# Sums of attention weights over four steps in every group, one of them by an adding transfer

## The chip, the cores and the metric

One core of a Trainium2 chip runs the kernel. The core has a matrix engine (TensorE, PE), a vector engine (VectorE, DVE), an activation engine (ScalarE, ACT), a general one (GpSimd, POOL) and a queue for transfers (SyncE, SP). Each works through its own list of instructions in order; semaphores tell one engine when another's result is there. The metric is device time in microseconds, the median of several executions.

## The reference

The input has 16 batches of 1024 nodes with 256 features and one adjacency matrix. Three graph-attention layers and one transformer layer follow each other, each with a layer norm and a rectifier ahead of it and a residual around it. The change lies in the transformer layer's attention, which has 8 heads of 32 features:

```python
scores = jnp.einsum('fnhd,fmhd->fhnm', q, k) / jnp.sqrt(jnp.asarray(D, x.dtype))
mask = (adj > 0)[None, None, :, :]
scores = jnp.where(mask, scores, jnp.asarray(-1000000000.0, x.dtype))
attn = jax.nn.softmax(scores, axis=-1)
t = jnp.einsum('fhnm,fmhd->fnhd', attn, v).reshape(F, N, C)
```

Layer norm, a two-layer network (256 to 256 to 256) and a second layer norm follow. A softmax needs, beside the weighted sum of the values, the sum of the weights of each row. That sum is what the change computes in another way.

## The kernel before, in words

`direct` writes the whole program down first and orders it afterwards. Each piece of work (some matmuls, an activation, a transfer) is recorded with its engine, an estimated duration, and the buffers that it reads and writes (`Record.add`). `Record.schedule` then plays these estimates through: for each engine it takes, of the pieces whose inputs are ready, the one with the lowest key. The key of a piece is its batch number plus a value interpolated in `KNOTS` at the piece's place in its stream, so that pieces of different batches and layers interleave: while one batch is in its attention, the next is in its graph layers and the one before in its feed-forward part. `PASS` is the time that a result is taken to need from one engine to the next. A transfer is recorded with two numbers: how long it occupies the transfer engines and how much later it lands; `SLACK` is added to that. These numbers only decide the order in which instructions stand in the engines' lists. The chip keeps that order and goes by its semaphores.

In `attention` (from L1084), for each of two groups of four heads (`g`), each half of the rows (`hf`) and each of eight column tiles (`jt`), one step does this:

- PE multiplies queries and keys, one matmul a head, into four score banks (L1355). Queries and keys come as high and low parts through DRAM (`project`, L1134 to L1158: an `hl` buffer is stored, then read back in four transfers).
- ACT takes the exponential of each head's scores into `pa` (L1379), a buffer with two heads side by side, 128 x 1024 elements; a step fills two of them, and six exist.
- DVE multiplies each by the adjacency mask (L1388).
- PE adds weights times values into one bank: a quad of four matmuls, one a head, each on a quarter of the array's columns (L1220, `bank<-pa,va`).
- For the sums of the weights PE multiplies the weights by a block of ones into another bank: again a quad (L1220, `bank<-sums,ones`).

The last item need not be done for each step, as weights of several steps can be added first. `run_of` gives the number of steps: 1 in the last batch, in which nothing is added; elsewhere 4 for the second half of the rows and 2 for the first. With 2, DVE adds the two steps' weights into a buffer `sums` (L1247, two additions of 128 x 1024) and one quad follows. With 4, DVE adds the first two, and for the third and the fourth step a transfer each, issued by POOL, adds the weights to `sums` in SBUF (L1256, two transfers of 512 KB a step; the fourth's waits for the third's on the same `sums`). Then comes the quad.

At the end of a batch (`feed`) the residual is read from DRAM into `xr` (L1505), the second layer norm's result is added, and the sum is stored. These transfers, the queries' and keys', and the graph layers' rows all stand in SP's one list. Names in the profile: `qs` and `ks` are queries and keys, `sc` a score bank, `va` the values, `pt`, `row` and `qb` belong to the graph layers (L870, L897, L984), `xh` holds a batch's features.

Of the kernel before, what the change touches and what calls it, by code (L numbers as in the profile page):

```python
# [113 lines left out]


WEIGHT = {"pe": 1.0, "dve": 0.3}
PASS = {"pe": 0.122, "act": 0.556, "dve": 0.232, "pool": 0.13, "dma": 0.0}


class Work:  # L120
# [23 lines left out]
class Record:  # L144
# [135 lines left out]


BEHIND, HELD = 2.0, 1.35
SLACK = 0.722
KNOTS = {
    "gat0": (-10.926, -10.742, -7.218, -4.626, -2.628, -2.099, -0.444, -3.636, -2.816),
    "gat1": (0.191, 0.25, 0.454, 0.45, 0.566, 0.582, 0.633, 1.016, 0.672),
    "gat2": (1.126, -0.076, -0.221, -0.062, 0.894, -0.428, 0.959, 1.018, 1.17),
    "beside": (1.093, 3.374, 4.836, 2.176, 5.971),
    "values": (1.444, -1.53, -3.682, -3.253, 0.902, 0.891, 2.874, 0.851, 0.421),
    "steps": (0.98, 1.188, 1.323, 1.512, 1.578, 1.712, 2.006, 2.02, 1.489),  # L290
    "feed": (2.026, 2.163, 1.768, 1.658, 2.343, 1.828, 2.009, 2.223, 3.042),
    "last": (3.521, -0.495, 0.103, 1.329, 1.339, 5.969, 5.585, 3.41, 5.439),
}
BIAS = 2.241
LEAD = {"act": 8.212, "dve": 0.635}

SWITCH = {
    ("full", "col4"): 0.137,
# [11 lines left out]
def tt_us(n):  # L310
    return (n / 0.96 + 67) / 1000
# [17 lines left out]
def direct(ctx, tc, flag, x, adj, gat_w, gat_a, w_qkv, ln1_g, ln1_b, ln2_g, ln2_b, w1, b1, w2, b2, out):  # L329


    nc = tc.nc
    NB, N, C = x.shape
# [92 lines left out]
    def dve(us, emit, w, r):  # L426
        rec.add("dve", us, emit, w, r)
# [4 lines left out]
    def dma(moved, lands, emit, w, r, key=None, us=0.57, engine="dma"):  # L432
        rec.add(engine, us, emit, w, r, key=key, moved=moved, lands=lands)
# [293 lines left out]
    def gat(xt, b_mv, b_rstd, l, my):  # L727
# [120 lines left out]
        def spread(hf, h, rd):  # L848

            row = my.row.new()  # L850
            dma(
                1.2,
                2.07,
                lambda: nc.sync.dma_start(
                    row.t,
                    rd.t[h * TH : (h + 1) * TH, :]
                    .rearrange("t n -> (t n)")
                    .partition_broadcast(P),
                ),
                [row],  # L860
                [rd],
            )
            return row
# [220 lines left out]
    def attention(b, xt, b_mv, b_rstd):  # L1084
# [42 lines left out]
        def project(g, hf, keys, stack, at):  # L1127

            sc, hi, lo = r_sc.new(), r_hi.new(), r_lo.new()
            c0 = keys * C + g * P  # L1130

            def product():
                for ct in range(CT):
                    nc.tensor.matmul(  # L1134
                        sc.t,
                        wqkv_sb[:, ct, c0 : c0 + P],
                        hT.t[:, ct, hf * HALF : (hf + 1) * HALF],
                        start=ct == 0,
                        stop=ct == CT - 1,
                    )  # L1140

            pe(CT * mm_us(HALF), product, [sc], [b_qkv] + [hT((ct, hf)) for ct in range(CT)])
            act(act_us(HALF), lambda: nc.scalar.copy(hi.t.bitcast(F32R), sc.t), [hi], [sc])  # L1143
            dve(
                tt_us(HALF),
                lambda: nc.vector.tensor_sub(lo.t, sc.t, hi.t),
                [lo],
                [sc, hi],
            )
            hl = r_hl.new()  # L1150
            for k, part in enumerate((hi, lo)):
                dma(0.65, 1.5, lambda: nc.sync.dma_start(hl.t[:, k, :], part.t), [hl(k)], [part])
            for a in range(4):
                k = ((0, 0, 1, 1), (0, 1, 0, 1))[keys][a]
                dma(
                    1.0,
                    1.83,
                    lambda: nc.sync.dma_start(  # L1158
                        stack.t[a * D3 : (a + 1) * D3, :, at : at + HALF],
                        hl.t[:, k, :].rearrange("(r d) n -> d r n", r=HG),  # L1160
                    ),
                    [stack((r, hf if keys else 0, a)) for r in range(HG)],
                    [hl(k)],
                )
# [62 lines left out]

        def run_of(g, hf):

            return 1 if b == NB - 1 else 4 if hf == 1 else 2  # L1230

        rec.stream(b, KNOTS["steps"])
        GROUP = 2
# [1 line left out]
        for n in range(len(steps) + LAG):  # L1235
            m = n - LAG
            if m >= 0:
                g, hf, jt = steps[m]
                if jt == 0:
                    accs[g, hf] = [r_bank.new(), r_bank.new()]  # L1240
                run = run_of(g, hf)
                if jt % run == 1:
                    sums[g, hf] = [r_sums.new() for _ in range(2)]
                    for ss, p0, p1 in zip(sums[g, hf], pas[m - 1], pas[m]):
                        dve(
                            tt_us(2 * HALF),
                            lambda: nc.vector.tensor_add(ss.t, p0.t, p1.t),  # L1247
                            [ss],
                            [p0, p1],
                        )  # L1250
                elif jt % run:
                    for ss, pt in zip(sums[g, hf], pas[m]):
                        dma(
                            2.8,
                            0.85,
                            lambda: nc.gpsimd.dma_start(ss.t, pt.t, accum_op=ALU.add),  # L1256
                            [ss],
                            [pt],
                            us=1.135,
                            engine="pool",  # L1260
                        )
                pe(
                    0.8585,
                    lambda: quad(
                        accs[g, hf][0],
                        lambda r: pas[m][r // 2].t[:, r % 2, :],
                        lambda r: va.t[:, jt, (g * HG + r) * D3 : (g * HG + r + 1) * D3],
                        jt == 0,
                        jt == NT - 1,
                    ),  # L1270
                    [accs[g, hf][0]],
                    pas[m] + [va(jt)],
                    ("col4", "col4"),
                )
                if jt % run == run - 1:
                    ss = pas[m] if run == 1 else sums[g, hf]
                    pe(
                        0.8585,
                        lambda: quad(
                            accs[g, hf][1],  # L1280
                            lambda r: ss[r // 2].t[:, r % 2, :],
                            lambda r: ones,
                            jt == run - 1,
                            jt == NT - 1,
                        ),
                        [accs[g, hf][1]],
                        ss,
                        ("col4", "col4"),
                    )
# [111 lines left out]
    def feed(b, x3, hn):  # L1401
# [95 lines left out]
        def back(hf):  # L1497
            yT = yTs[hf]
            for it in (hf * TH, hf * TH + 2):
                g, z, mvz, rstdz = r_bank.new(), r_fz.new(), r_mvz.new(), r_rstdz.new()  # L1500
                xr = r_xr.new()
                dma(
                    1.0,
                    1.83,
                    lambda: nc.sync.dma_start(xr.t, x3.t[:, it : it + 2, :]),  # L1505
                    [xr(0), xr(1)],
                    [x3(hf)],
# [763 lines left out]
```

## Time and profile before

| | |
|---|---|
| Median of 3 runs | 4077.2 us (4068.3 to 4077.9) |
| Profiled execution, device time | 4072.0 us |
| Its span, first to last instruction | 4070.3 us |
| PE busy | 4012.3 us, 99% |
| DVE busy | 3501.7 us, 86% |
| ACT busy | 2666.6 us, 66% |
| POOL busy | 621.0 us, 15% |
| DMA engines, mean rate | 112 GB/s |
| TensorE clock granted | 0.995 |

The profile is one execution. Its page gives busy time and share of the span for each engine; "PEld" is PE's loading of weights, which overlaps its matmuls. Groups of instructions are named by source line, engine and operation, with what they write and read, the count, busy time in microseconds, the mean of one in nanoseconds, and then the engine's idle time just before them and what ended most of it. Matmuls in fp32 appear as two records each. The ends of matmuls are modelled, so times from one start to the next say more of PE than durations. The chain of waits is followed back from the last instruction, at each step to what released it.

### The profile page before, as it was taken

Reading aid. Unit: us, or ns where it says so; the run is one execution under the profiler, and the core shown is the slowest. Engines: PE = TensorE matmul, PEld = TensorE weight load, DVE = VectorE, ACT = ScalarE, POOL = GpSimd, SP = SyncE. Lnnn points to the kernel's source line nnn. Section 1 sums busy time; section 2 is a strip of 40 time slices with the busy share of each in tenths; the row PEclk is TensorE's granted clock in tenths of the full one; section 3 lists DMA queues with packets and bytes.
Section 4 is the critical chain, followed back from the end, with each engine's and each line's share of the span. In section 5 each row is a group of like instructions: output and inputs, shape, how many; then the busy total and the mean of one; then the engine's idle time right before and its main releaser. Section 6 shows DMA issues by size and latency. Waiting matters only on the chain.

```text
span 4070.3 us, 66071 instructions
## 1 busy us (share of the span) xinstructions
PE 4012.3 (99%) x23874; PEld 2352.0 (58%) x23874; DVE 3501.7 (86%) x5994; ACT 2666.6 (66%) x6673; POOL 621.0 (15%) x631
## 2 busy tenths in 40 slices
PE   7999999999999999999999999999999999999998
PEld 4566466564655646566564665646556465665643
DVE  7778898989989899898988989899898998989866
ACT  5467575775757767576675766757577675766765
POOL 1101111111111112111111111111111121111200
PEclk9999999999999999999999999999999999999999
DMA  3034454444545345463444544445543454624451
GB/s 128 27 103 115 126 126 109 113 104 115 124 125 123 83 117 126 115 150 76 126 110 123 127 110 113 104 115 122 127 121 82 117 128 115 150 69 121 112 137 51
DMA packets 227520, 456.54 MB, mean 112 GB/s; under 512 B 24688, under 2 KB 59760, under 8 KB 227184
## 3 DMA queue, kind: packets, MB, share of 16 engines
q1 hardware_dynamic: 192624, 326.39, 28.3%
q0 software_dynamic: 34560, 125.84, 16.2%
q8 instruction: 190, 3.11, 0.3%
q14 instruction: 146, 1.20, 0.1%
HBM read 225.25 MB, written 101.06 MB: 80 GB/s over the span
## 4 chain that ended last, share of the span: by engine, by line
PE 94%; DMA 3%; ACT 1%; DVE 1%; issue 0%; SPq 0%; DVEq 0%; ACTq 0%; POOLq 0%
PE bank L897 21%; PE bank L1220 16%; PE sc L1355 12%; PE bank L984 11%; PE bank L772 9%; PE bank L531 6%; PE sc L1134 5%; PE bank L1452 5%; PE bank L994 5%; PE sc L1172 3%; DMA sums<-pa 2%; PE sc L531 1%; DVE pt L870 1%; ACT waste L448 0%; ACT pa L1379 0%
## 5 line engine op out<-in xcount | busy, mean ns | idle before, releaser
L1388 DVE TENSOR_TENSOR pa<-pa,mask 128x1024 f32<-128x1024 f32 x1024 | 1222.7, 1219 | 166.1 <-ACT pa L1379 162.6
L1379 ACT ACTIVATE pa<-sc 128x512 f32<-128x512 f32 x2048 | 1101.6, 611 | 370.1 <-DVE sums L1247 174.4
L870 DVE SCALAR_TENSOR_TENSOR pt<-row,e,mask 128x512 f32<-128x512 f32 x1472 | 1011.9, 744 | 46.6 <-DMA row<-rd 27.7
L897 PE MATMUL bank<-qb,pt 128*128 128x257 f32 x4096 | 941.0, 380 | 0.0
L897 PEld LDWEIGHTS bank<-qb,pt 128*128 128x128 f32 x4096 | 770.6, 190 | 143.6 <-issue 20.1
L1355 PE MATMUL sc<-qs,ks 128*128 128x512 f32 x2048 | 727.9, 457 | 2.6 <-DMA hl<-hi 1.1
L1220 PE MATMUL bank<-pa,va 128*32 128x512 f32 x4096 | 515.0, 597 | 0.0
L1355 PEld LDWEIGHTS sc<-qs,ks 128*128 128x128 f32 x2048 | 361.3, 189 | 237.9 <-ACT pa L1379 82.5
L984 PE MATMUL bank<-pt,qb 128*32 128x512 f32 x3840 | 461.7, 596 | 6.5 <-DVE pt L870 6.5
L1247 DVE TENSOR_TENSOR sums<-pa,pa 128x1024 f32<-128x1024 f32 x360 | 434.1, 1220 | 16.7 <-PE bank L1220 14.2
L772 PE MATMUL bank<-w_aug,hT 128*128 128x259 f32 (+1 forms) x1504 | 373.3, 389 | 0.0
L1256 POOL DMA_DIRECT2D sums<-pa x240 | 211.5, 883 | 954.1 <-DVE pa L1388 426.6
L772 PEld LDWEIGHTS bank<-w_aug,hT 128*128 128x128 f32 x1504 | 280.3, 190 | 99.6 <-ACT qb L794 35.4
L925 ACT ACTIVATE ex<-bank,rec 128x256 f32<-128x256 f32 x256 | 121.4, 475 | 288.9 <-DVE rec L917 288.7
L984 PEld LDWEIGHTS bank<-pt,qb 128*32 128x32 f32 x3840 | 116.5, 110 | 294.8 <-issue 219.5
L1220 PEld LDWEIGHTS bank<-pa,va 128*32 128x32 f32 x4096 | 115.0, 109 | 250.6 <-issue 225.7
L994 PE MATMUL bank<-pt,e 128*32 128x512 f32 x1920 | 252.0, 593 | 0.1
L1134 PE MATMUL sc<-hTa,wqkv_sb 128*128 128x512 f32 x512 | 240.0, 596 | 0.0
L468 POOL TENSOR_TENSOR rstd<-rstd,neg_half 128x4 f32<-128x4 f32 x96 | 169.2, 1762 | 362.1 <-DVE rstd L460 362.0
L1143 ACT CAST hi<-sc 128x512 fp32r<-128x512 f32 x128 | 75.1, 587 | 211.8 <-PE sc L1134 122.0
L502 ACT ACTIVATE hn<-xh,mv,rstd 128x256 f32<-128x256 f32 x376 | 202.8, 613 | 7.5 <-DVE mv L492 4.1
L1220 PE MATMUL bank<-sums,ones 128*32 128x512 f32 x1440 | 200.5, 600 | 3.9 <-DMA sums<-pa 3.7
(152 smaller groups left out, 4501.0 us busy)
## 6 DMA issues: line engine op xcount, KB each, us to landing
sums<-pa POOLq DMA_DIRECT2D x240, 512.0 KB, 6.0
ks<-hl SPq DMA_DIRECT2D x256, 256.0 KB
qs<-hl SPq DMA_DIRECT2D x256, 256.0 KB
row<-rd SPq DMA_DIRECT2D x184, 256.0 KB
hl<-hi SPq DMA_DIRECT2D x128, 256.0 KB
hl<-lo SPq DMA_DIRECT2D x128, 256.0 KB
xh<-in_x_dram SPq DMA_DIRECT2D x32, 512.0 KB
x<-xh SPq DMA_DIRECT2D x32, 512.0 KB
```

The costliest lines, as they stand in the source:

```text
L531: nc.tensor.transpose(dst(k), src(k), ident[:shape, :shape])
L772: nc.tensor.matmul(g.t[:, : C + 3 * H], hT.t[:, ct, k * P : (k + 1) * P], w_aug[l][:, ct, :], start=ct == 0, stop=ct == CT - 1,)
L870: lambda: nc.vector.scalar_tensor_tensor(pt.t, row.t, e3[:, 2, jt // TH, h, jt % TH : jt % TH + 1], mask[:, jt, hf * HALF : (hf + 1) * HAL ...
L897: nc.tensor.matmul(g.t[:, : D + 1], pts[jt].t[:, k * P : (k + 1) * P], qb[:, jt, 0, :], start=jt == 0, stop=jt == NT - 1,)
L984: nc.tensor.matmul(g.t[u * D + d : u * D + d + D3, :], qb[:, j, h + u, d : d + D3], pts[u][j - jt].t, start=j == 0, stop=j == NT - 1,)
L994: nc.tensor.matmul(gd.t[c : c + D3, :], one(jt + k, h + u).to_broadcast([P, D3]), pts[u][k].t, start=jt == 0, stop=jt == NT - 2,)
L1134: nc.tensor.matmul(sc.t, wqkv_sb[:, ct, c0 : c0 + P], hT.t[:, ct, hf * HALF : (hf + 1) * HALF], start=ct == 0, stop=ct == CT - 1,)
L1220: nc.tensor.matmul(ac.t[r * D3 : (r + 1) * D3, :], columns(r), of_head(r), start=first, stop=last,)
L1247: lambda: nc.vector.tensor_add(ss.t, p0.t, p1.t),
L1355: nc.tensor.matmul(scs[r - r0].t, ks.t[:, r, jt * P : (jt + 1) * P].bitcast(F32R), q.t[:, r, :].bitcast(F32R), start=True, stop=True,)
L1379: lambda: nc.scalar.activation(pt.t[:, v, :], sc.t, AF.Exp, scale=1.0 / math.sqrt(D3)),
L1388: lambda: nc.vector.tensor_mul(pt.t, pt.t, mask[:, jt : jt + 1, i0 : i0 + HALF].to_broadcast([P, 2, HALF]),),
```

## The change

Three things change in the program.

1. `run_of` gives 4 in every batch but the last, for both halves of the rows. The first half no longer goes in pairs.
2. In a run of 4, the first two steps are added by DVE as before, the third step's weights by an adding transfer as before, and the fourth step's weights by DVE, to the same `sums`, when the transfer has landed. The fourth step's transfer is gone.
3. The scheduler's numbers are fitted anew: `PASS`, `SLACK`, all `KNOTS`, `BIAS`, `LEAD`, and the two numbers of five kinds of transfer. They move instructions in the engines' lists and add none.

In the order as built, the matmul instructions with ones on summed weights go from 720 to 480 (each is two records in the profile), DVE's additions for the sums from 360 to 480, and the adding transfers stay at 240. The lists of all engines differ over their whole length.

```diff
-PASS = {"pe": 0.122, "act": 0.556, "dve": 0.232, "pool": 0.13, "dma": 0.0}
+PASS = {"pe": 0.146, "act": 0.223, "dve": 0.215, "pool": 0.13, "dma": 0.0}
...
-SLACK = 0.722
+SLACK = 0.871
 KNOTS = {
...
-    "values": (1.444, -1.53, -3.682, -3.253, 0.902, 0.891, 2.874, 0.851, 0.421),
-    "steps": (0.98, 1.188, 1.323, 1.512, 1.578, 1.712, 2.006, 2.02, 1.489),
-    "feed": (2.026, 2.163, 1.768, 1.658, 2.343, 1.828, 2.009, 2.223, 3.042),
-    "last": (3.521, -0.495, 0.103, 1.329, 1.339, 5.969, 5.585, 3.41, 5.439),
+    "values": (-0.174, -0.634, -1.621, -1.921, -0.925, 0.988, 7.017, 0.066, 0.002),
+    "steps": (0.679, 1.306, 1.313, 1.627, 1.731, 1.892, 2.245, 2.072, 0.464),
+    "feed": (2.531, 3.778, 2.14, 2.018, 2.622, 2.047, -0.257, 0.785, 3.186),
+    "last": (1.057, 1.904, 1.664, 0.156, 2.035, 2.203, 2.695, 3.982, 5.043),
 }
-BIAS = 2.241
-LEAD = {"act": 8.212, "dve": 0.635}
+BIAS = 2.353
+LEAD = {"act": 5.778, "dve": -2.572}
...
             dma(
-                1.2,
-                2.07,
+                1.45,
+                1.75,
                 lambda: nc.sync.dma_start(
                     row.t,
...
-                dma(0.65, 1.5, lambda: nc.sync.dma_start(hl.t[:, k, :], part.t), [hl(k)], [part])
+                dma(0.82, 1.67, lambda: nc.sync.dma_start(hl.t[:, k, :], part.t), [hl(k)], [part])
...
                 dma(
-                    1.0,
-                    1.83,
+                    1.15,
+                    2.18,
                     lambda: nc.sync.dma_start(
                         stack.t[a * D3 : (a + 1) * D3, :, at : at + HALF],
...
         def run_of(g, hf):
 
-            return 1 if b == NB - 1 else 4 if hf == 1 else 2
+            return 1 if b == NB - 1 else 4
...
+                elif run == 4 and jt % run == 3:
+                    for ss, pt in zip(sums[g, hf], pas[m]):
+                        dve(
+                            tt_us(2 * HALF),
+                            lambda: nc.vector.tensor_add(ss.t, ss.t, pt.t),
+                            [ss],
+                            [pt],
+                        )
                 elif jt % run:
                     for ss, pt in zip(sums[g, hf], pas[m]):
                         dma(
-                            2.8,
-                            0.85,
+                            2.4,
+                            2.0,
                             lambda: nc.gpsimd.dma_start(ss.t, pt.t, accum_op=ALU.add),
...
                 dma(
-                    1.0,
-                    1.83,
+                    1.3,
+                    1.6,
                     lambda: nc.sync.dma_start(xr.t, x3.t[:, it : it + 2, :]),
```

## The prediction

> **What bounds the kernel now.** I read the page's busy shares first, then its costliest groups, then busy time by stretch, and last the chain of waits and the timelines of single engines where the change touches them. The page:
>
> ```profile
> span 4070.3 us, 66071 instructions
> PE 4012.3 (99%) x23874; PEld 2352.0 (58%) x23874; DVE 3501.7 (86%) x5994; ACT 2666.6 (66%) x6673; POOL 621.0 (15%) x631
> ...
> PE 94%; DMA 3%; ACT 1%; DVE 1%; issue 0%; SPq 0%; DVEq 0%; ACTq 0%; POOLq 0%
> ...
> L1247 DVE TENSOR_TENSOR sums<-pa,pa 128x1024 f32<-128x1024 f32 x360 | 434.1, 1220 | 16.7 <-PE bank L1220 14.2
> ...
> L1256 POOL DMA_DIRECT2D sums<-pa x240 | 211.5, 883 | 954.1 <-DVE pa L1388 426.6
> ...
> L1220 PE MATMUL bank<-sums,ones 128*32 128x512 f32 x1440 | 200.5, 600 | 3.9 <-DMA sums<-pa 3.7
> ...
> sums<-pa POOLq DMA_DIRECT2D x240, 512.0 KB, 6.0
> ```
>
> PE is 99% busy and holds 94% of the chain; DVE comes next with 86%. The three groups that the change touches are the VectorE adds (360), the adding transfers (240) and the matmuls with the ones (1440 records, 8 to a quad, so 180 quads). Busy time by stretch (length, then busy time of PE, weight loads, DVE, ACT, POOL) shows where PE is not full:
>
> ```profile
> 0.00:142.80 142.80, 118.09 (x847) 60.44 (x848) 117.86 (x242) 75.30 (x216) 14.41 (x22) 0.94 0.31 101
> ...
> 2105.54:2351.84 246.30, 246.30 (x1479) 145.81 (x1479) 218.57 (x373) 165.41 (x417) 40.19 (x40) 1.00 0.47 116
> 2351.84:2599.59 247.75, 247.34 (x1479) 145.94 (x1479) 218.57 (x373) 165.47 (x417) 39.82 (x40) 1.00 0.47 115
> ...
> 3831.70:4070.30 238.60, 211.38 (x1126) 105.81 (x1125) 156.45 (x257) 144.46 (x332) 26.77 (x26) 0.94 0.36 92
> ```
>
> The middle of the kernel repeats every 247 us, one batch to a period, with PE busy throughout. Of PE's 58 us of idle time in the whole span (4070.3 - 4012.3), 25 lie in the start and 27 in the last stretch. So time comes off only by taking work off PE, or in those two ends. DVE has 247 - 218.6 = 28 us of idle time in a period. The chain of waits in order of time prices a quad, because there each piece runs from one start to the next:
>
> ```profile
> 2118.65 2.71 PE bank L1220 x24
> ...
> 2143.19 1.00 PE bank L1220 x8
> ...
> 2241.59 3.57 PE bank L1220 x32
> ```
>
> Three quads take 2.71, four take 3.57: one more costs 0.86 us. One alone, with the turn into the quadrant layout and out of it, costs 1.00. (200.5 / 180 = 1.11 is a quad's whole modelled length, which overlaps its neighbours.) A VectorE add is priced in the same way from DVE's timeline; the second is followed at once, 1.13 us after it starts:
>
> ```profile
> 2249.53 1.23 DVE L1247 TENSOR_TENSOR sums<-pa,pa 128x1024 f32<-128x1024 f32 x1 [0.21 <-PE bank L1220]
> ...
> 2252.94 1.22 DVE L1247 TENSOR_TENSOR sums<-pa,pa 128x1024 f32<-128x1024 f32 x1
> 2254.07 3.49 DVE L1388 TENSOR_TENSOR pa<-pa,mask 128x1024 f32<-128x1024 f32 x3
> ```
>
> In the last stretch the chain names one long transfer, with SyncE's queue ahead of it:
>
> ```profile
> 3897.99 3.47 DMA out_dram<-xr
> 3903.26 7.90 DMA qs<-hl
> 3911.20 2.08 PE sc L1355 x4
> ```
>
> **What the Trainium skill says.** VectorE: DVE Perf Modes, section on the perf-mode tier table: an fp32 tensor_tensor runs in the slowest mode only; its errata section gives (N + 151)/0.96 ns, an estimate of 1224 ns for 1024 elements. The trace agrees: 1220. PSUM — Partial Sum Buffer, section Engine vs sequencer instructions: VectorE's queue is strictly first in, first out, so an add that waits for a transfer holds all VectorE work behind it. No line of this trace shows such a case, since no add waits for a transfer yet. DMA: Bandwidth & Descriptors, Anatomy of one DMA: 2.0 us plus bytes over 436 GB/s, an estimate of 3.2 us for 512 KB. The trace differs: 6.0 us median, 4.4 to 9.8 over the 240; I use the trace.
>
> **The change part by part.** The sum is made against the profiled execution, 4072.0 us (span 4070.3); the runs' median, 4077.2, is 5 us above it, their lowest 4 below.
>
> *Quads removed.* In 15 batches the first half of the rows (hf 0) went in pairs: 4 quads with the ones for each of two head groups, now 2. That is 4 fewer a batch, 60 in all (180 to 120). At 0.86 to 1.00 each: 52 to 60 us; most stand beside another quad, so I take 0.88, **-53 us**, all on PE's path.
>
> *Turns.* In the order as built PE enters the quadrant layout 413 times before and 388 times after. 25 fewer at 1.00 - 0.86 = 0.14: **-3 us**.
>
> *VectorE adds.* For one head group of one batch, hf 0 had 4 pairs of 2 tiles, 8 adds; now 2 pairs and 2 fourths of 2 tiles, 8 again. hf 1 had 2 pairs, 4 adds; now 8. So 24 a batch become 32, 360 become 480. 120 x 1.13 = 136 us of VectorE, 9.8 us busy a batch at 1.22. DVE goes from 218.6 of 247 us (88%) to 228.4 of about 243.4 (94%), and its idle time from 28 to 15 us. The cover is PE: while PE sets the pace an add costs nothing. Bounds: at best 0; at worst all 28 us of DVE's present idle time is forced and stays, and a period is 228.4 + 28 = 256 us, 9 above today. Today's waits of DVE are mostly for ACT's exponentials and PE's results, which come earlier when PE runs faster, so most of that idle time gives way. I take **+10 us** for places where adds crowd (0.7 a batch).
>
> *Transfers.* Still 240 of 512 KB: hf 1 loses half of its 16 (two in a row on one sum, the second waiting for the first), hf 0 gains 8. Each group of four now has one in its chain, then an add. Work of DVE that stands between the last input of a transfer and the add that waits for it, counted in the order as built at these rows' prices, is 4.3 to 15.2 us with a median of 7.7; for 45 of the 240 it is under 6.0, the median landing. In a steady batch these are the three or four with 4.7, 5.7 and 6.0 us, short by 1.3, 0.3 and little: 2 to 3 us of DVE a batch, within its 15 and inside the +10 above. What waits behind is mask multiplications, and through them PE's quads. PE itself no longer waits for transfers of sums: its 3.7 us go, and weight loads' 13. ACT's waits for buffers read by such a transfer (41.7 us) and by an add (174.4) were no PE time; a fourth step's buffer is now held until its add.
>
> *The refit.* New knots and costs move work of all engines but add no instruction; SyncE issues 1271 transfers in both. In the middle nothing can be gained, as PE is full. At the end something can: before, the queries' transfers of the last batch (four, issued from 3901.9) stood in SyncE's queue behind two output stores and two loads of residuals that waited for VectorE; PE was busy 11.3 of the 19.3 us from 3894 to 3913.3. In the new order these four follow their own stores directly, ahead of those. Bounds: 8 us gained, or nothing and a new gap of like size elsewhere; I take **-5**. Start: same instructions, PE waits for setup; 0, within 5 either way.
>
> Sum: -53 - 3 + 10 - 5 = -51: 4072 - 51 = **4021 us**.
>
> **Rivals.** *Partly given back:* crowded adds and late landings cost PE 2 to 3 us a batch rather than 0.7: 15 x 1.5 to 2.5 more, 4043 to 4062. For it: 94% of DVE in a queue that can't pass a waiting add; landings of up to 9.8 us. Against it: three quarters of the adds have over 6.6 us of other work ahead. *VectorE becomes the bound (slower):* the 16 adds of a batch that wait at the queue's head. PE's new need is 243.4 us a batch. If half of DVE's present idle time is forced (14 us), 228.4 + 14 leaves 1 us, and the group breaks even with today's 247 at 4.6 us more, so at 4.6/16 = 0.3 us of uncovered wait for each of the adds; at 1.0 us each a period is 258 us, 11 over today: 4072 + 15 x 11 - 8 (turns and the end) = about 4230; at 0.5 us, about 4115. For it: landings vary between 4.4 and 9.8 us. Against: in today's periods DVE's waits follow a PE that is never late. *More gain:* nothing is given back and the end's gap closes: 4072 - 60 - 3 - 8 = 4001. *The change does nothing of what it says* is excluded: the order as built has 480 matmul instructions with the ones on summed weights where it had 720.
>
> **Chances.** Forecast (4003 to 4042) 0.53; partly given back (4042 to 4066) 0.22; more gain (below 4003) 0.08; VectorE the bound 0.17, of which some 0.03 near no change. A measurement of this kernel tells 0.3%, 12 us, from no change. Faster 0.79, same 0.07, slower 0.14. The range 3999 to 4066 leaves out the slower rival and the last of the gain, 0.2 together; the forecast's own is 4003 to 4042.
>
> **What would show it.** Right: 960 records in the group with the ones at 0.86 to 1.00 us a quad in the chain; periods of 243 to 244.5 us with PE busy throughout and DVE near 228; adds of the fourth step waiting for sums' transfers for under 3 us a batch; the end's gap before the last batch's first scores under 5 us. Wrong: PE idle in the middle, with waits for VectorE's sums or masked weights; DVE above 96% of a period; a median landing well above 6.0 us.

## The result

The changed kernel takes 4059.5 us (median of 6 runs, 4055.5 to 4065.3), the kernel before 4073.3 us (median of 6, 4068.3 to 4077.9). The ratio is 0.9969, with a 95% interval of 0.9958 to 0.9981: 13.8 us by the medians, where 4021 us was forecast, 51 below the profiled execution of before. The direction was right, the size was not.

The page of the changed kernel (span, busy time of each engine with its share of the span and its instructions, landing of the adding transfers):

```profile
span 4053.7 us, 64966 instructions
...
PE 3972.2 (98%) x23394; PEld 2337.5 (58%) x23394; DVE 3624.3 (89%) x6114; ACT 2670.9 (66%) x6673; POOL 641.4 (16%) x631
...
sums<-pa POOLq DMA_DIRECT2D x240, 512.0 KB, 4.9
```

And its groups of instructions by line (busy time, mean of one in ns, then the engine's idle time just before them and what ended it):

```profile
L1255 DVE TENSOR_TENSOR sums<-sums,pa 128x1024 f32<-128x1024 f32 x240 | 290.9, 1213 | 1.6 <-DMA sums<-pa 1.6
L1247 DVE TENSOR_TENSOR sums<-pa,pa 128x1024 f32<-128x1024 f32 x240 | 289.1, 1217 | 9.9 <-PE bank L1220 9.9
...
L1264 POOL DMA_DIRECT2D sums<-pa x240 | 213.9, 892 | 1464.5 <-DVE pa L1396 664.4 <-PE sc L1363 259.3 <-DVE sums L1247 233.3
...
L1220 PE MATMUL bank<-sums,ones 128*32 128x512 f32 x960 | 127.3, 597 | 0.5 <-DVE sums L1255 0.3 <-ACT hT L766 0.2
```

All parts of the change are there as counted: 960 records with the ones on summed weights instead of 1440, two times 240 additions on VectorE instead of 360, 240 transfers. The transfers land in 4.9 us instead of 6.0, and the additions of fourth steps (L1255) wait 1.6 us for them in the whole run. What is not there is the time. PE is busy 40.1 us less (4012.3 to 3972.2), but its idle time has grown from 58.0 to 81.5 us (4053.7 - 3972.2), so the span falls by 40.1 - 23.5 = 16.6 us only.

Busy time by stretch tells where that idle time is. I cut the span at two marks that repeat once a batch on PE (its first transposes of a batch's features): 13 whole periods lie between the first and the last cut. Columns as in the prediction: length, then busy time of PE, weight loads, DVE, ACT, POOL. The kernel before:

```profile
0.00:435.30 435.30, 407.80 (x2439) 246.97 (x2439) 336.38 (x635) 259.83 (x672) 49.39 (x61) 0.98 0.33 92
435.30:3649.10 3213.80, 3210.50 (x19218) 1896.82 (x19214) 2840.86 (x4835) 2145.45 (x5392) 517.42 (x520) 1.00 0.47 116
...
3649.10:4070.30 421.20, 393.98 (x2226) 208.22 (x2222) 324.43 (x526) 261.29 (x611) 54.22 (x52) 0.97 0.43 107
```

The changed kernel, with one single period between:

```profile
0.00:424.00 424.00, 391.10 (x2286) 238.77 (x2286) 330.30 (x622) 253.14 (x649) 46.75 (x60) 0.99 0.35 95
424.00:3629.60 3205.60, 3174.77 (x18802) 1886.50 (x18798) 2946.98 (x4941) 2153.48 (x5409) 535.48 (x520) 1.00 0.47 116
...
1409.20:1656.20 247.00, 244.19 (x1450) 145.12 (x1446) 226.68 (x381) 165.59 (x417) 41.38 (x40) 1.00 0.47 116
...
3629.60:4053.70 424.10, 406.32 (x2314) 212.25 (x2310) 347.00 (x553) 264.27 (x617) 59.18 (x51) 0.98 0.42 105
```

PE's idle time in the 13 middle periods was 3213.8 - 3210.5 = 3.3 us and is now 3205.6 - 3174.8 = 30.8 us. At the start it went from 27.5 to 32.9 us and at the end from 27.2 to 17.8 us (with 88 records of work moved into the end). So the end lost idle time, as was expected of it, and the middle gained it: a period takes 3205.6 / 13 = 246.6 us where it took 247.2. The forecast had 243.4 for PE's work alone and 244.1 with its 0.7 for crowded additions. VectorE is at 226.7 of 247 us, 92%, and has 20 us of idle time in a period.

PE's waits say what it waits for in the middle (total us, times, longest). One of each comes with nearly every batch, and neither is a wait for sums or masked weights:

```profile
PE bank L1460 <- ACT ex L925: 13.5, 13, 1.0
...
PE bank L531 <- DVE rec L917: 9.8, 11, 1.2
```

L1460 is the feed-forward part's matmul, L531 a helper for all transposes, here those of the feed-forward's result `yT`. `ex` and `rec` belong to the graph layers' softmax; they read a bank, and L1460 and L531 write one. The timeline of one period shows how the second of them arises (start, length, engine, and in brackets the idle time of the engine before it):

```profile
1288.41 0.49 SPq L1585 DMA_DIRECT2D out_dram<-xr  x1
...
1293.24 0.34 SPq L1513 DMA_DIRECT2D xr<-x  x1
...
1297.38 0.69 DVE L1519 TENSOR_TENSOR xr<-xr,row_c 128x512 f32<-128x512 f32 x1 [2.00 <-DMA xr<-x]
1297.99 0.16 DVE L917 RECIPROCAL rec<-bank 128x1 f32<-128x1 f32 x1
1298.19 0.47 ACT L925 ACTIVATE ex<-bank,rec 128x256 f32<-128x256 f32 x1 [7.59 <-DVE rec L917]
...
1299.05 0.75 DVE L1498 SCALAR_TENSOR_TENSOR yT<-bank,col_b,yT 128x512 f32<-128x512 f32 x1
```

The output's store from `xr` is issued at 1288.41; the next residual's load goes into the same buffer, of two, and is issued at 1293.24, after a wait for the store's landing. VectorE reaches the addition that needs it (L1519) 2.00 us too early and waits at the head of its queue. Behind it stand a reciprocal for which ACT waits, the feed-forward's sum `yT` (L1498, ended at 1299.80), which PE's transposes read, and the next reciprocal, which the profile names as the last that they waited for: they start at 1299.94, after 0.95 us of idle time. The Trainium skill (PSUM — Partial Sum Buffer, section Engine vs sequencer instructions) calls VectorE's queue strictly first in, first out; this wait agrees with it. The prediction saw no such case in the profile of before, and that holds for additions to `sums` alone: the residual's load held VectorE there too, five times and 12.5 us in all. It hardly did so in the middle. VectorE's waits for it in the 13 periods, first before and then after the change:

```profile
DVE xr L1511 <- DMA xr<-x: 0.5, 1, 0.5
...
DVE xr L1519 <- DMA xr<-x: 23.5, 20, 2.0
```

### The profile page after: what moved, and what is told of

Its sections match the earlier page's. It is cut to its first block, busy times and chain, and to the rows that moved or that the text cites. A ratio compares the mean times of both kernels' runs of the same rounds, so it can differ in the third digit from the quotient of the medians.

```text
span 4053.7 us, 64966 instructions
## 1 busy us (share of the span) xinstructions
PE 3972.2 (98%) x23394; PEld 2337.5 (58%) x23394; DVE 3624.3 (89%) x6114; ACT 2670.9 (66%) x6673; POOL 641.4 (16%) x631
## 5 line engine op out<-in xcount | busy, mean ns | idle before, releaser
L897 PEld LDWEIGHTS bank<-qb,pt 128*128 128x128 f32 x4096 | 769.3, 189 | 178.6 <-ACT ota L1303 12.6
L1363 PE MATMUL sc<-qs,ks 128*128 128x512 f32 x2048 | 739.3, 463 | 3.5 <-ACT pa L1387 3.4
L772 PE MATMUL bank<-w_aug,hT 128*128 128x259 f32 (+1 forms) x1504 | 373.8, 390 | 0.7 <-ACT hT L766 0.7
L772 PEld LDWEIGHTS bank<-w_aug,hT 128*128 128x128 f32 x1504 | 276.7, 190 | 112.9 <-issue 33.6
L1247 DVE TENSOR_TENSOR sums<-pa,pa 128x1024 f32<-128x1024 f32 x240 | 289.1, 1217 | 9.9 <-PE bank L1220 9.9
L1255 DVE TENSOR_TENSOR sums<-sums,pa 128x1024 f32<-128x1024 f32 x240 | 290.9, 1213 | 1.6 <-DMA sums<-pa 1.6
L1015 ACT COPY ot<-bank 128x512 f32<-128x512 f32 x120 | 68.5, 582 | 276.0 <-PE bank L984 262.9
L448 ACT ACTIVATE waste<-xh,mv 128x256 f32<-128x256 f32 x384 | 196.1, 511 | 7.2
```

What stands on the lines that cost most here:

```text
L772: nc.tensor.matmul(g.t[:, : C + 3 * H], hT.t[:, ct, k * P : (k + 1) * P], w_aug[l][:, ct, :], start=ct == 0, stop=ct == CT - 1,)
L897: nc.tensor.matmul(g.t[:, : D + 1], pts[jt].t[:, k * P : (k + 1) * P], qb[:, jt, 0, :], start=jt == 0, stop=jt == NT - 1,)
L1255: lambda: nc.vector.tensor_add(ss.t, ss.t, pt.t),
L1363: nc.tensor.matmul(scs[r - r0].t, ks.t[:, r, jt * P : (jt + 1) * P].bitcast(F32R), q.t[:, r, :].bitcast(F32R), start=True, stop=True,)
```

## The experiments

In all of them the order of instructions in the engines' lists stays as in the kernel that they start from, unless said. "Over one column" means that an instruction stays in its place with its waits and works on one column of each head, of 512. In the kernels with short quads, and in the kernel before with short additions, some additions of VectorE ahead of full quads also add 0.001, in one fused instruction that takes as long (1220 ns in the mean, where the plain additions beside it take 1222); the diffs below leave that out. Two runs of one kernel can differ by 10 us, so a few us between two medians are read with care.

### Fewer additions, or fewer quads, in the changed kernel

Theory A: the 240 new additions crowd VectorE. Theory B: they don't, and the loss lies elsewhere.

```diff
-                            lambda: nc.vector.tensor_add(ss.t, ss.t, pt.t),
+                            lambda: nc.vector.tensor_add(ss.t[:, :, :1], ss.t[:, :, :1], pt.t[:, :, :1]),
```

> The changed kernel with its order of instructions kept, but each of the 240 adds of the fourth step's weights reaches over one column of each of its two heads instead of 512, so those weights are missing from the sums. It takes 240 x about 1.1 us, 17 us a batch, off VectorE and leaves PE, ACT and the transfers as they are. Theory A (the adds crowd VectorE, and what they delay reaches PE through ACT): the 3 us a batch that went missing come back, periods of 243 to 244 us, 4015 to 4030 us in all. Theory B (the waits are in the order that the refitted numbers made, whatever VectorE has to do): within 10 us of the changed kernel's 4059.

Measured: 4052.9 us, ratio to before 0.9957 (0.9941 to 0.9974), 6.5 us below the changed kernel by the medians, with intervals that overlap. VectorE was busy 219 us less (3405.0 of 4049.5 us, 84%), and the 13 middle periods stayed at 246.5 us on average, from 246.6. The missing time does not come back, so theory A falls as its account. PE's list of waits shows that the additions had nevertheless made one of its two waits:

```profile
PE bank L531 <- DVE rec L917: 16.2, 13, 2.0
...
PE bank L1460 <- DVE yT L1498: 5.5, 8, 1.2
```

The wait for `ex` at L1460 (13.5 us) is gone from it. Laid record by record beside the changed kernel's, PE's starts gain 12.6 us there over the 13 periods and lose 11.9 us at the transposes of `yT` and at the next feed-forward product. VectorE's list says what stands ahead of those:

```profile
DVE xr L1519 <- DMA xr<-x: 67.1, 31, 3.5
```

Its wait for the residual's load doubled from 31.6 us: VectorE comes to the same place earlier and waits there for the same transfer. One wait replaced the other.

The counterpart takes work from PE: 60 of the 120 quads with the ones over one column.

```diff
-                    of_head(r),
+                    of_head(r)[:, :n],
...
-                            jt == run - 1,
-                            jt == NT - 1,
+                            jt == run - 1 or (run == 4 and jt == 7),
+                            jt == NT - 1 or (run == 4 and jt == 3),
+                            1 if run == 4 and jt == 3 else HALF,
```

> The changed kernel, order kept, with 60 of its 120 quads with the ones (the first of each two in a half) reaching over one column; those weights are missing from the sums. PE has 60 x 0.8 = 48 us less to do. If PE's own work still fills the period: 4012 us. If waits for VectorE and ACT fill it: 4050 us or more.

Measured: 4056.0 us, ratio 0.9961 (0.9947 to 0.9975): 3.5 us, not clear of noise, for 48 us of PE's work. Then PE's work does not set the period either.

### The same two in the kernel before

If that is so in the changed kernel, was it so before, where PE was 99% busy? Here 60 of the 180 quads go over one column, as if the change had removed them, and the order is not touched.

> The kernel before with its order kept, but the 60 quads that the change removes (the first of each two pairs in hf 0) multiply one column instead of 512; those pairs are missing from the sums. VectorE's work stays as before. If PE's time in the middle was its own work, as the prediction had it: 60 x 0.86 to 0.88 less, so 4073 - 52 = 4021 us. If PE was also paced by ACT and VectorE, with waits hidden under the modelled ends of its matmuls: less than half of it, 4045 us or more.

Measured: 4075.0 us over 20 runs, ratio 1.0004 (0.9997 to 1.0011). Nothing came off. Its page (busy time, then the shares of the chain of waits):

```profile
PE 4012.1 (98%) x23874; PEld 2346.6 (57%) x23874; DVE 3499.0 (86%) x5994; ACT 2667.4 (65%) x6673; POOL 621.2 (15%) x631
...
PE 74%; DVE 12%; DMA 5%; ACT 4%; issue 3%; POOL 2%; SPq 0%; DVEq 0%; POOLq 0%; ACTq 0%
```

PE shows 4012.1 us of busy time where it showed 4012.3 with 48 us more to do. (The profiled execution was the slowest of the twenty, 4084.3 us; its span is 12.1 us longer than in the profile of before, and its idle time 12.3.) The ends of matmuls are modelled: a quad has two rounds of four records, a record lasts 592 ns, and where nothing waits the next round starts 0.43 us after the last, so a wait of up to some 0.16 us leaves no gap. The Trainium skill (Perfetto Trace Analysis, section Identifying the Most-Contended Engine) says that matmul busy time is not a good measure of how close a kernel is to its limit. This pair agrees, although here busy time says too much, while the section's reason is that pipelined instructions look smaller in a trace. The share of weight loads, one of the two measures that the section names instead, was 58% and is 57% here. The chain says more: 94% of it was PE, now 74%, some of which may be the slower execution. The timeline shows what becomes of the time:

```profile
1502.55 0.22 PE L1220 MATMUL bank<-sums,ones 128*32 128x1 f32 x8
1502.61 1.90 PE L1220 MATMUL bank<-pa,va 128*32 128x512 f32 x16
...
1509.23 0.62 PE L1220 MATMUL bank<-sums,ones 128*32 128x512 f32 x2 [0.39 <-DVE sums L1247]
```

The short quad's successor starts 0.06 us after it instead of 0.86, and within a few steps PE stops for the next sum (VectorE's addition L1247) or the next masked weights, and the 0.8 us are gone.

So VectorE looks as late as PE in these steps. The next two runs make the 120 additions of the same pairs short, alone and together with the quads.

```diff
-                            lambda: nc.vector.tensor_add(ss.t, p0.t, p1.t),
+                            lambda: nc.vector.tensor_add(ss.t[:, :, :1], p0.t[:, :, :1], p1.t[:, :, :1])
+                            if run == 2 and jt % 4 == 1
...
```

> The kernel before, order kept, with VectorE's 120 additions of the first pairs short and all quads at full length; those pairs' weights are missing from the sums, whose quads read what the buffer holds. If PE's own work fills the period: no change, 4066 to 4078 us. If VectorE sets the pace in the first half's steps: 1 to 2 us a batch less, 4045 to 4060 us.

> The kernel before, order kept, with the 60 quads of the first pairs short as in the second experiment and VectorE's 120 additions of the same pairs reaching over one column a head as well; those weights are missing from the sums. If PE's saved time was eaten by VectorE's additions and masks in the same place: PE's 3.2 us a batch show now, 4020 to 4035 us. If another chain sets the period: 4055 us or more.

Measured: additions alone 4070.5 us, 0.9994 (0.9987 to 1.0001); both 4047.4 us, 0.9930 (0.9914 to 0.9947). About 0 from the quads, 3 from the additions (not clear of noise), 26 together. In the kernel before two chains of about equal length ran side by side through the attention's first half: PE's matmuls and VectorE's masks and additions. Shortening either alone leaves the other. What held back the rest of the quads' 48 us was not looked into.

### The numbers without the sums, the sums without the numbers

> The sums of the change (fours everywhere, fourth step added by VectorE) with all numbers of the scheduler as before. Theory A: VectorE is as crowded, so no faster than the changed kernel: 4055 to 4090 us. Theory B: the refit brought the waits, so the old numbers show the gain of the sums alone: 4020 to 4035 us.

> The sums of the kernel before with all numbers of the scheduler as changed. The start and the end gained about 11 and 9 us and the period before the end lost 12 in the changed kernel; if the refit brings that whatever the sums, 4065 us by theory A, the middle's period staying at 247 us. Theory B: the refit's order brings its 3 us a batch of waits here too, with no quads saved: 4090 to 4110 us.

Measured: new sums with the old numbers 4211.1 us, 1.0342 (1.0324 to 1.0359), periods of 257 us; old sums with the new numbers 4239.9 us, 1.0417 (1.0399 to 1.0434), periods of 232, 250 and 297 us in turn. Both are far slower than either full kernel, and than any of the theories had. The chain of waits of the first, shares by engine:

```profile
PE 54%; DVE 25%; DMA 7%; ACT 7%; issue 4%; POOL 2%; SPq 0%; DVEq 0%; POOLq 0%; ACTq 0%
```

VectorE holds a quarter of it, with no more work than in the changed kernel (3618.5 us busy). The order decides that, by some 150 us; the refit is no trimming at the ends but a part of the change. The first stretch up to the second mark (424.0 us after the change, 435.3 before) needs both as well: 436.3 and 452.8 us here.

### The residual's load

Theory C: the load at the head of VectorE's queue (the timeline above) sets the period. The first test lets the output be computed and stored from `fz`, so that `xr` is free earlier.

```diff
-                            xs, u, rstdz.t[:, k : k + 1], xs, op0=ALU.mult, op1=ALU.add
+                            u, u, rstdz.t[:, k : k + 1], xs, op0=ALU.mult, op1=ALU.add
...
-                        out[b].rearrange("(t p) c -> p t c", p=P)[:, it : it + 2, :], xr.t
+                        out[b].rearrange("(t p) c -> p t c", p=P)[:, it : it + 2, :], z_t
```

> The changed kernel with its order kept, but the last operation of the second layer norm writes its result into the buffer fz that it reads, and the output is stored from there. The next load of a residual into the same xr then need not wait until the store has landed. Theory C (two waits of each period set the pace: VectorE stands at its queue's head for the residual's transfer, and the reciprocals and yT behind it come late to ACT and PE): those 2 us a batch go, 13 x 2 = 26 less, 4025 to 4040 us. Rival (the order as a whole is bound by several chains of about the same length, so one wait taken out comes back at the next): 4048 us or more.

> The last one and the short adds of the fourth steps together (these weights are missing from the sums), the order kept. Theory C with VectorE's work as the second chain: both waits of the period gone, periods of 243 us, about 4015 us. Rival (other chains just behind): over 4040 us.

Measured: 4068.7 us, 0.9988 (0.9981 to 0.9995), 9 slower than the changed kernel; with short additions as well 4077.9 us, 1.0011 (1.0002 to 1.0020). VectorE's wait for the load fell to 1.5 us, and ACT's list of waits has a new one in its place:

```profile
ACT fz L1481 <- DMA out_dram<-fz: 40.0, 13, 3.4
```

The store's landing now holds `fz`, which ACT needs for the feed-forward's first activation; PE's wait at the transposes is gone, and at L1460 it waits 20.4 us for `fz` instead. The wait was moved and not removed, so this does not decide on theory C.

The second test is a third buffer for `xr`. Its room comes from a scratch tile made of bytes and from the block of ones, which becomes a broadcast of one column.

```diff
+    xr_tiles = r_xr.tiles + ring("xr_more", 1, [2, C]).tiles
+    xr_count = [0]
...
-    ones = work.tile([P, D3], F32, name="ones")
-    nc.gpsimd.memset(ones, 1.0)
+    ones = ones_col.to_broadcast([P, D3])
...
+                xr.t = xr_tiles[xr_count[0] % 3]
+                xr_count[0] += 1
```

> The changed kernel, order kept, with a third buffer for the residuals, so that a load waits for the store of two loads ago and no longer for the last one. Room for it comes from a discarded output of ACT in one byte an element and from the ones as a broadcast column. Theory C (the residual's load at the head of VectorE's queue sets the pace): 4025 to 4040 us. Rival (several chains of about the same length): 4050 to 4060 us, no more than a fifth of a microsecond a batch gained.

> The third residual buffer and the short adds of the fourth steps together (those weights are missing from the sums), order kept. If VectorE's work and the residual's load were the two chains that replaced each other: both waits of a period go, about 2 us a batch, 4015 to 4030 us. If PE or another chain stands just behind: over 4040 us.

> The changed kernel, order kept, with the third residual buffer, the short adds and the 60 short quads together (weights missing from the sums). If the period is the longest of a few chains through PE, VectorE and the residual's load, taking from all of them shows what each alone did not: 3 us a batch and more, 4000 to 4020 us. If yet another chain (ACT's order, the transfers of keys and queries) holds it: over 4035 us.

Measured: 4096.1, 4094.3 and 4089.8 us (1.0061, 1.0050 and 1.0036), all slower. This was a fault of the edit. It deals three buffers out in the order in which the pieces are recorded, but the planner runs them in another and knows only that piece k + 2 follows piece k. A buffer was so loaded again ahead of its last use (these kernels therefore add some residuals to the wrong rows), and new waits for loads stood in VectorE's queue. They test nothing, and are told because the next run is the same idea done rightly: the first buffer stays as it is, and the pieces that had the second take it in turns with the new one.

```diff
-                xr.t = xr_tiles[xr_count[0] % 3]
+                xr.t = xr_tiles[(1, 0, 2, 0)[xr_count[0] % 4]]
```

> The changed kernel with its order kept, and a third buffer for the residual in the feed-forward part: the records that had the second buffer now take it in turns with the new one, so the dependences between records of one buffer still hold in the order as built. (The room comes from a scratch tile made of bytes and from the block of ones, which becomes a broadcast.) The load no longer waits for the landing of the store just ahead of it in SyncE's list. Theory C, the residual's load at the head of VectorE's queue sets the period: the wait before xr (31.6 us in the changed kernel) falls below 8, PE's waits for ex and rec go with it, and the time is 4059 - 13 x 2.4 = about 4030. Theory D, PE's chain and VectorE's chain are of about equal length and neither alone sets it: within 8 us of 4059.

Measured: 4042.8 us, ratio 0.9932 (0.9915 to 0.9948), 16.6 us below the changed kernel. It leaves nothing out, and it beats both kernels. VectorE's list of waits, the line of the load into the two old buffers (into the third it is 1.2 us more):

```profile
DVE xr L1523 <- DMA xr<-x: 8.0, 13, 1.6
```

Busy time by stretch, the 13 middle periods:

```profile
423.60:3617.40 3193.80, 3172.12 (x18802) 1887.27 (x18798) 2946.72 (x4942) 2153.50 (x5409) 535.86 (x520) 1.00 0.48 116
```

The 13 periods are 11.8 us shorter than in the changed kernel (3205.6 to 3193.8). PE's wait at the transposes (9.8 us) is gone; its wait at L1460 (13.5 us) is unchanged. Laid record by record beside the changed kernel's, PE's starts differ in the middle at one place alone that counts: 12.0 us less ahead of the transposes of `yT`. The two edits that make the room do not show (ACT busy 2670.7 us where it was 2670.9, weight loads 2337.9 where they were 2337.5). So theory C holds for one of the two waits, and the load was worth about 0.9 us a period and 17 us in all, not the 29 that were expected of it.

### What is left

> The same third buffer, and in addition the 240 additions of fourth steps over one column instead of 1024, which leaves out most of their sum. Theory C: as in the kernel with the buffer alone, about 4030, since VectorE had time enough. Theory D: VectorE is relieved twice and PE not at all; PE's unstalled work of 227.6 us and its short waits remain, so 4045 to 4055, little below what the short additions gave alone (4053).

> The changed kernel with its order and its two residual buffers kept; the 240 additions of fourth steps and 60 of its 120 quads with the ones each over one column, which leaves out most of their work. Each alone took off 6.5 and 3.5 us. Theory D: both together take off much more than the 10 us of their sum, as in the kernel before (0 and 3 apart, 26 together): 4059 - 25 to 40 = 4020 to 4035. Theory C: the load's wait is untouched and the two together give what they gave apart, about 4049.

> All three: the third residual buffer, the 240 additions and 60 of the 120 quads over one column, which leaves out most of their work. Theory C: PE follows its work, 4030 - 48 = about 3982. Theory D: 4000 to 4030, below the kernel with both short by what the load's waits were worth once the other two chains are shorter.

Measured: third buffer and short additions 4036.0 us, 0.9909 (0.9892 to 0.9925); short additions and quads with two buffers 4048.4 us, 0.9942 (0.9925 to 0.9958); all three 4030.8 us, 0.9900 (0.9884 to 0.9917). The second of them is the one that decides: 11 us together, as 6.5 and 3.5 apart, and not the 25 to 40 of theory D. In the changed kernel additions and quads are no longer a balanced pair, and theory D, which was right for the kernel before, falls. All three together are the sum of their parts, 17, 7 and 5 us, far from the 3982 us of theory C. The additions are worth 6.5 us with two buffers and 6.9 with three. That is not all that hangs on them: with three buffers too PE's wait for `ex` at L1460 goes when they are short, 12.7 us over the 13 periods, but 6.4 us come back at the next feed-forward product, and VectorE's wait for the load is back at 40 us (37.7 for the old buffers, 2.7 for the third).

What stands between 245.7 us and the forecast's 243.4? The last two runs take VectorE out of the way: with the third buffer, all 1024 mask multiplications over one column.

```diff
-                                    mask[:, jt : jt + 1, i0 : i0 + HALF].to_broadcast(
-                                        [P, 2, HALF]
+                                    mask[:, jt : jt + 1, i0 : i0 + 1].to_broadcast(
+                                        [P, 2, 1]
```

> The kernel with the third residual buffer (4042.8 us), its order kept, and the 1024 mask multiplications of VectorE over one column in place of 512 a head, which leaves out nearly all of the masking: about 64 x 1.15 = 74 us of VectorE less in a batch, so that VectorE can pace nothing. Theory F, what is left of PE's waits stands behind VectorE's queue: the period falls from 245.6 by several us, 4042.8 - 13 x 3 to 6 = 3965 to 4005. Theory G, the pace is PE's own from here, with weight loads and score banks: within 10 us of 4043.

> The same, and 60 of the 120 quads with the ones over one column, which leaves out most of their work, about 0.8 us each and 48 in all. Where PE paces the kernel once VectorE is out of its way (F and G alike), the 48 us come off in full: 40 to 48 below the kernel with the short masks alone. If a third chain (ScalarE, transfers) paces it, under 15 come off.

Measured: 4004.4 us, 0.9834 (0.9817 to 0.9850), and with 60 quads short as well 3997.8 us, 0.9819 (0.9803 to 0.9836). The 13 middle periods of the first:

```profile
425.60:3584.20 3158.60, 3157.87 (x18802) 1886.63 (x18798) 2140.45 (x4941) 2151.66 (x5409) 445.90 (x520) 1.00 0.48 118
```

Each of the 13 is now 243.0 us to a tenth, and PE's idle time in all of them together is 0.7 us. PE's wait for `ex` at L1460 is gone from its list: 15.9 of the 35 us came off there, 7.1 at and right behind transposes of `hn`, the rest in small pieces. Theory F holds, at the edge of its range (2.7 us a period, where 3 to 6 were expected). The short masks also shorten the way from an exponential to PE's products, by about 1.1 us each; whether that or the emptier queue did it, the run does not tell. Two periods of the second run:

```profile
1162.00:1404.50 242.50, 241.23 (x1447) 144.37 (x1446) 164.41 (x381) 165.01 (x416) 34.32 (x40) 1.00 0.49 118
1404.50:1647.00 242.50, 241.41 (x1447) 144.45 (x1446) 164.49 (x381) 164.91 (x416) 34.33 (x40) 1.00 0.48 118
```

48 us less of PE's work, 6.6 us less of time: a period of 242.5 us stands with PE waiting in it and VectorE at 68%. So there is a third chain at 242.5 us. Whether PE's own work or this chain set the 243.0 us is not told, and that 243.0 is close to the forecast's 243.4 proves nothing for the forecast: its 243.4 was today's period less the quads, and today's period was not PE's work alone. Beside the run without short quads, PE gives back about half of the saved time ahead of and within the graph layers' products (L772 in the changed kernel), which take ACT's `hT`, and the rest in many small pieces. Which chain that is was not isolated and stays open.

## Why the prediction was wrong

**Quads removed: the step that failed.** "At 0.86 to 1.00 each", "all on PE's path": the count and the price were right and the path was not. An estimate from the traces (each matmul given the usual time from its start to the next start in its place, stalls left out) puts PE's unstalled time per period some 4 us lower (2.4 to 4.9, by what is taken as usual), as the 4 quads and the turns should give. The same estimate is 234 to 241 us a period in the changed kernel (227.6 by the choice of an expectation above), so even 243 us would hold small stalls. PE's pace was not only its own. In the kernel before, 48 us of the same quads were worth 0, and in the changed kernel half of its quads are worth 3.5. I read "PE 99%" and "PE 94%" as the proof that PE's work sets the time. The first is blind to small waits, and the second names one longest chain, not the next one, which was VectorE's and about as long.

**Turns.** Part of the same sum, with the same fault; the size is not told apart by any run.

**VectorE adds: size near by luck, reason wrong.** 10 us were taken for 120 crowded additions; making 240 short gives 6.5, and that number hides a larger wait that the load's wait replaced. The failed part is the sentence that VectorE's idle time "gives way", since its waits "come earlier when PE runs faster". It has 20 us of idle time a period and not 15, and yet it holds PE up: with the load's wait gone and the masks short, a period falls by 2.7 us (245.7 to 243.0, 35 us over 13). Short additions in place of short masks give 0.5 us a period (6.9 / 13), with the load's wait back in the way. What the waits show is a reciprocal or a sum for another engine behind other work in a queue that is 92% full. At L1460 the additions were enough to make the wait (12.7 of 13.5 us); which pieces of the queue make up the rest was not taken apart.

**Transfers.** Harmless, as said, and over-priced: 2 to 3 us of VectorE a batch was expected, 1.6 us in the whole run was measured, with landings of 4.9 us instead of 6.0. The long wait at the head of VectorE's queue was another transfer's, the residual's, that the prediction looked at only at the end of the kernel: 12.5 us of wait before, 31.6 after (0.5 and 23.5 in the 13 periods), worth 17 us by the third buffer. The new order brought that wait into the middle.

**The refit.** The gap at the end closed as said: from 3885 to 3912 us PE is busy throughout, and its idle time in the end fell by 9.4 us; with the work moved into it the end is 2.9 us longer. The start, taken as 0 within 5, is 11.3 us shorter, but with 16.7 us less of PE's work in it and 5.4 us more of idle time. The sentence "in the middle nothing can be gained, as PE is full" had it the wrong way round: with the new sums and the old numbers the middle takes 257 us a period.

**The sum.** Of the forecast's 51, about 35 did not come. In the middle it had 40 us (13 periods of 244.1 in place of 247.2) and 8 came; start and end together had 11 and gave 8.4. The load (11.8 us over the 13 periods) and the rest of what the short masks take away (35.2) are more than the 32 that are missing in the middle, as the third buffer and the short masks on top of it show one after the other. The time lies in the stated range of the rival that had part of the gain given back (4043 to 4062), but that range was reckoned too high: 2 to 3 us a batch in place of 0.7 is 1.3 to 2.3 more, 4041 to 4056, and even its own 1.5 to 2.5 ends at 4058.5. Of its two causes late landings were none, and crowded additions made one of PE's two waits; the other cause, the residual's load, it did not have. The rival in which VectorE becomes the bound named the right engine; its price, 16 uncovered waits a batch for transfers of sums, did not occur.

## What to carry to other kernels

A busy share of 99% and a chain that names one engine do not say that its work sets the time: ask for the second chain, and test it by making a piece of that engine's work short in place, before a forecast counts on it. Take work from two engines one by one and together: here that gave 0, 3 and 26 us before the change and 3.5, 6.5 and 11 after it. Lay two traces of one order beside each other record by record: a wait that goes at one place and comes back at the next shows there and not in the total. Look for the transfer at the head of an in-order queue: what stands behind it may belong to other engines. An order fitted to one set of work was of no use for another (here 150 us and more), so the sums and their order are one change.

## What was not expected of the hardware

Taking 48 us of matmuls out of PE left its busy time as the profile counts it unchanged to 0.2 us (4012.3 and 4012.1). The 512 KB adding transfers landed in 4.6 us in the median when none was in flight at their issue, in both kernels, and in 6.1 (before) and 6.0 us (after) when the last one still was; before the change 160 of the 240 were of the second kind, after it 73, and that makes the medians of 6.0 and 4.9. A load waited for the store of the same buffer to land, not to be issued: 4.8 us lay between the two issues in the timeline shown (1288.41 to 1293.24), and SyncE's list of waits puts 4.3 of them down to the store's landing.
